# One set of score matmuls per group in layer 1 of a two-layer graph attention kernel, with k held twice

## The chip, the cores and the metric

The kernel runs on one core of a Trainium2 chip. The metric is the device time of the whole program in microseconds. The program is one launch that computes both layers. Five engines run their own instruction streams and meet at semaphores: TensorE (PE, with its weight loads shown apart as PEld), VectorE (DVE), ScalarE (ACT), GpSimd (POOL), and SyncE (SP), whose queue issues all DMAs here.

## What is computed

The input `x` has 128 graphs of 64 nodes with 768 features, `adj` a boolean 64x64 matrix per graph. Everything is fp32.

```python
# layer 0: 12 heads of 64, additive attention, gate, layer norm
h    = einsum('bnd,ade->bane', x, W);  th = tanh(h)
attn = leaky(th @ w_src + (th @ w_dst).T);  attn = where(adj, attn, -999)
feat = elu(softmax(attn) @ h + b)
gate = sigmoid(x @ H_w.T + H_b)
x    = layernorm(x + gate * feat + (1 - gate) * x)
# layer 1: 6 heads of 128, dot-product attention, layer norm
q, k, v = heads(x @ Wq + bq), heads(x @ Wk + bk), heads(x @ Wv + bv)
scores  = einsum('bhqd,bhkd->bhqk', q, k) / sqrt(128)
probs   = softmax(scores + where(adj, 0, -9e15))
x       = layernorm(x + (probs @ v merged over heads) @ Wf + bf)
```

The change concerns the scores of layer 1 and three buffers around them.

## The kernel before

Two graphs of 64 nodes fill the 128 partitions, so the input is 64 tiles of 128 tokens. `phase_a` computes layer 0 for 32 pairs of tiles, and with the product `Wv` also v of layer 1; it leaves the layer norm's rows, their transposes and v in DRAM. `phase_b` computes layer 1 for 16 groups of four tiles, two pairs `q` of two tiles `i` each. The weights of both phases use the same three SBUF tiles `w0`, `w1`, `w2`, of 7 x 3 x 384 = 8064 fp32 per partition. In `phase_b` they hold Wq, Wk and Wf, each as 15 blocks of 2 x 256 (`weight15`), 7680 of the 8064.

The products with Wq, Wk and Wf are written with 15 block products in place of 18 (`STEPS`): each step multiplies one combination of input blocks with one combination of weight blocks into one of four PSUM accumulators, and then adds the accumulator to, or subtracts it from, one or more output blocks. The combinations of the input are made by POOL: `sum_of_group` for the group's transposed input `T4` (tiles S0 to S10), `pair_sum` for the transposed contexts (tiles Sc0 to Sc10). `Stream.step` issues a step: two matmuls of 256 columns (L896), then the reads of PSUM. For q and k (`start_qk`) the first read of an output block is an ACT instruction (L917) and the further ones are DVE additions (L922). For the last product (`start_f`) all are DVE additions to the residual rows `xs` (L939). Pools rotate their buffers: a tile that is allocated again waits for the last reader of the buffer it gets.

A group takes six streams of 15 steps. Steps 0 to 59 of a group are q of the even heads (half j = 0), k of j = 0, q of j = 1, k of j = 1. In steps 60 to 89 the same positions hold the last product of the group before, first for its pair q = 0 and then for q = 1; so the streams of consecutive groups follow each other without a gap on PE. The other work is hung on step numbers by `at(step, f)`: `run` goes through the steps and calls first the dense step of that number and then the functions at it. This order is that of every engine's queue, because the whole is scheduled by hand.

For a group beginning at step o, the parts that the change touches or passes are these:

- `scores(d, 0)` at o + 32 and `scores(d, 1)` at o + 62, each two steps after the last step of that half's k. For each of three pairs of heads `nb` it allocates a PSUM tile `pb` and issues 8 matmuls (L961), one for each pair of tiles, tile and graph. Each multiplies the 128 features of 64 queries with 64 keys, and goes to the upper or lower 64 partitions.
- `scores_read` (L969) at o + 33, 35, 37 and o + 63, 65, 67 (o + 63, 64, 65 for the second half of the last group). Two DVE instructions per `nb` scale the scores, add the mask term `fill`, and write them to the softmax tiles `s0`, `s1`.
- `fill` at o + 26 makes the mask term from `adj`.
- The softmax from o + 95 (o + 66 in the last group); `probs` transposes the probabilities on PE (L1016) and ACT copies them to `pt` (L1022); `contexts` multiplies them with v (L1040) and DVE reads the result to `cT` (L1054).
- `pair_sum` (L878) for q = 0 from o + 113 and for q = 1 from o + 151, that is in steps 23 to 43 and from step 61 of the next group's numbering; `load_x` and `add_bf` (L863) bring in the residual rows; `load_T4` at step 61 and `sum_of_group` (L285) from step 66 prepare the next group.

The parts that set the order for the scores are these lines:

```python
b0 = o + (2 * j + 2) * R + 2
at(b0, lambda d=d, j=j: scores(d, j))
for nb in range(3):
    at(b0 + 1 + (1 if last and j else 2) * nb, lambda d=d, j=j, nb=nb: scores_read(d, j, nb))
```

q is allocated with two buffers and k with one, so k of the second half overwrites k of the first.

Of the kernel before, what the change touches and what calls it, by code (L numbers as in the profile page):

```python
# [9 lines left out]
F32 = mybir.dt.float32  # L10
U8 = mybir.dt.uint8
AF = mybir.ActivationFunctionType
ALU = mybir.AluOpType
AX = mybir.AxisListType

P = 128
# [45 lines left out]
def kernel(  # L62
# [31 lines left out]
    nc = tc.nc  # L94
    NB, S, D = x.shape
    A, _, E = W.shape
    HEADS = 6
    DH = D // HEADS
    NC = D // P
    HALF = D // 2  # L100
    CH = NC // 2
# [9 lines left out]
    wts = ctx.enter_context(tc.tile_pool(name="wts", bufs=1))  # L111
# [32 lines left out]
    def weight_tile(tag):  # L144
        return wts.tile([P, 7, CH, HALF], F32, name=f"w{tag}", tag=f"w{tag}")

    def weight15(i):
        return wts.tile([P, 7, CH, HALF], F32, name=f"w{i}", tag=f"w{i}").rearrange(
            "p s c o -> p (s c o)"
        )[:, : 15 * 2 * 256].rearrange("p (s c o) -> p s c o", s=15, c=2)  # L150

    def load15(wb, src, k):

# [123 lines left out]
    def group_part(d, r):  # L277

        if r < 6:
            return T4[:, :, r // 3, 2 * (r % 3) : 2 * (r % 3) + 2, :]  # L280
        return d["S"][r - 6]
# [42 lines left out]
    def phase_a(ctx):  # L324
# [470 lines left out]
        def load_early(i, src, k):  # L795
            if len(early) == i:
                early.append(weight15(i))
            load15(early[i], src, k)
# [16 lines left out]
    def phase_b(ctx, wq, wk, early_sums):  # L815
        NG = NP // 2
        k1 = ctx.enter_context(tc.tile_pool(name="l1", bufs=1))
        k3 = ctx.enter_context(tc.tile_pool(name="l3", bufs=1))
        small = ctx.enter_context(tc.tile_pool(name="lsmall", bufs=2))
        psb = ctx.enter_context(tc.tile_pool(name="psb", bufs=4, space=bass.MemoryType.PSUM))  # L820
# [15 lines left out]
            d["adj"] = a  # L836

        def fill(d):
            d["fill"] = small.tile([P, 2, 2, S], F32, name="fill1")
            nc.vector.tensor_scalar(  # L840
                d["fill"], d["adj"], 1.0, -L1_NEG, op0=ALU.subtract, op1=ALU.mult
            )
# [26 lines left out]
        def pair_part(d, q, r):  # L869

            if r < 6:
                return d["c", q, r // 3][:, 2 * (r % 3) : 2 * (r % 3) + 2, :]
            return d["Sc", q, r - 6]

        def pair_sum(d, q, k):
            r0, r1, op = SUMS[k]
            t = k1.tile([P, 2, P], F32, name=f"Sc{k}")
            nc.gpsimd.tensor_tensor(t, pair_part(d, q, r0), pair_part(d, q, r1), op)  # L878
            d["Sc", q, k] = t

# [29 lines left out]

        def start_qk(d, name, w, bias, j):

            o = k1.tile([P, 6, 2, P], F32, name=name, bufs=2 if name == "q" else 1)

            def first(b, positive, ps):
                hd = 2 * (b % 3) + j
                nc.scalar.activation(  # L917
                    o[:, b], ps, AF.Identity, bias=bias[:, hd : hd + 1], scale=1.0 if positive else -1.0
                )

            def add(b, positive, ps):
                nc.vector.tensor_tensor(o[:, b], o[:, b], ps, ALU.add if positive else ALU.subtract)  # L922

            d[name] = Stream(
                lambda r, slot, c: w[:, slot, c, j * P : (j + 1) * P],
                lambda r, slot, c: (
                    dup[:, DUP[r]] if d is st[0] and r in DUP else group_part(d, r)
                )[:, :, c, :],
                [P, 2, P],
                first,  # L930
                add,
            )
            d[name + "T", j] = o
# [13 lines left out]
            )  # L947


        def scores(d, j):  # L950
            if j == 0:
                d["s"] = [k3.tile([P, 2, HEADS, S], F32, name=f"s{q}") for q in range(2)]
            qT, kT = d["qT", j], d["kT", j]
            for nb in range(3):
                pc = psb.tile([P, 2, 2, S], F32, name="pb")
                for q in range(2):
                    for i in range(2):
                        for gr in range(2):
                            own = slice(gr * S, (gr + 1) * S)
                            b = 3 * i + nb  # L960
                            nc.tensor.matmul(  # L961
                                pc[own, q, i, :], qT[:, b, q, own], kT[:, b, q, own],
                                start=True, stop=True,
                            )
                d["pc", nb] = pc

        def scores_read(d, j, nb):
            for q in range(2):
                nc.vector.scalar_tensor_tensor(  # L969
                    d["s"][q][:, :, 2 * nb + j, :], d["pc", nb][:, q], 1.0 / math.sqrt(DH),  # L970
                    d["fill"][:, q], op0=ALU.mult, op1=ALU.add,
                )

        def sm_part(d, q, i):
            return d["s"][q][:, i]
# [36 lines left out]
        def probs(d, q, i):  # L1012

            ps = psb.tile([P, CH, P], F32, name="pb")
            for j in range(CH):
                nc.tensor.transpose(  # L1016
                    ps[:, j, :],
                    d["s"][q][:, i, 2 * j : 2 * j + 2, :].rearrange("p h m -> p (h m)"),
                    ident,
                )  # L1020
            d["pt", i] = k3.tile([P, CH, P], F32, name="pt", bufs=2)
            nc.scalar.copy(d["pt", i], ps)  # L1022

        def contexts(d, q):
# [71 lines left out]
        def at(step, *fs):  # L1096
            events.setdefault(max(step, 0), []).extend(fs)

        def at_first(step, f):

            dense.setdefault(step, []).append(f)

        R = len(STEPS)
# [21 lines left out]
        for g in range(NG):  # L1125
            d, o = st[g], N * g
            d["S"] = {} if g else early_sums
            last = g == NG - 1
            if g:
                at(o - 29 if g > 1 else 14, lambda g=g: load_T4(g))  # L1130
                at(o - 35, lambda g=g: load_adj(g))
            at(o + 26, lambda d=d: fill(d))
            ready = {}
            for k in sorted(range(len(SUMS)), key=need) if g == 0 else range(len(SUMS)):
# [6 lines left out]
                if g == 1:  # L1141

                    t = max([R * 3 + SUM_STEPS[k] + 2] + [ready[r] for r in SUMS[k][:2] if r in ready])
                    ready[6 + k] = t
                else:
                    t = o - 24 + 2 * k
# [4 lines left out]
            for j in range(2):  # L1151
                for n, (name, w, bias) in enumerate((("q", wq, bq_c), ("k", wk, bk_c))):
                    b0 = o + (2 * j + n) * R
                    at_first(b0, lambda d=d, a=(name, w, bias, j): start_qk(d, *a))
                    for i in range(R):
                        at_first(b0 + i, lambda d=d, name=name, i=i: d[name].step(i))
                b0 = o + (2 * j + 2) * R + 2
                at(b0, lambda d=d, j=j: scores(d, j))
                for nb in range(3):
                    at(b0 + 1 + (1 if last and j else 2) * nb, lambda d=d, j=j, nb=nb: scores_read(d, j, nb))  # L1160

            sm = o + 4 * R + 6 if last else o + N + 5
            for q in range(2):
                f = o + ((6 if last else 10) + q) * R
                for i in range(2):

                    t = sm + 4 * i + 13 * q if last else sm + 3 * i + 8 * q
                    at(t + (2 if last else 4), lambda g=g, q=q, i=i: load_v(g, q, i))
                    if last:
                        at(t, lambda d=d, q=q, i=i: sm_top(d, q, i, True))  # L1170
                        at(t + 2, lambda d=d, q=q, i=i: sm_top_exp(d, q, i))
                        at(t + 5, lambda d=d, q=q, i=i: sm_scale_act(d, q, i))
                        at(t + 8, lambda d=d, q=q, i=i: probs(d, q, i))
                        if i:
                            at(t + 11, lambda d=d, q=q: contexts(d, q))
                        continue
                    at(t, lambda d=d, q=q, i=i: sm_top(d, q, i))
                    at(t + 1, lambda d=d, q=q, i=i: sm_sub(d, q, i))
                    at(t + 3, lambda d=d, q=q, i=i: sm_exp(d, q, i))
                    at(t + 6, lambda d=d, q=q, i=i: sm_total(d, q, i))  # L1180
                    at(t + 7, lambda d=d, q=q, i=i: sm_scale(d, q, i))
                    at(t + 10, lambda d=d, q=q, i=i: probs(d, q, i))
                    if i:
                        at(t + 12, lambda d=d, q=q: contexts(d, q))
# [3 lines left out]
                for k in range(len(SUMS)):  # L1188
                    if q == 0:
                        t = pr + 10 + (k if last else 2 * k)  # L1190
                    else:

                        t = max(
                            [f - R + SUM_STEPS[k] + 1, pr + 10]
                            + [ready[r] for r in SUMS[k][:2] if r in ready]
                        )
# [7 lines left out]
                if last and q:  # L1204
                    for b in range(6):
                        t = f + max(i for i in range(R) if STEPS[i][5][b])
# [7 lines left out]
                for i in range(2):  # L1214
                    t = f + R + 1 + 2 * i
# [48 lines left out]
```

## Time and profile before

| | us |
|---|---|
| median of 3 runs | 2852.86 |
| lowest, highest | 2852.34, 2855.02 |
| the profiled execution | 2855.12 |
| its span from first to last instruction | 2853.3 |
| PE busy in the span | 2812.0 (99%) |
| DVE, POOL, ACT busy | 1856.9, 1543.3, 1198.7 |
| mean granted TensorE clock | 0.998 |
| one score matmul record (L961), median | 0.222 |
| one read of scores (L969), median | 0.282 |
| one addition to xs or k (L939, L922), mean | 0.42 |
| one Sc sum on POOL (L878), mean | 0.731 |

The page's times are those of one profiled execution. Its span begins and ends with an instruction, and the execution's own time is 1.8 us longer. Layer 0 takes about the first half of the span and layer 1 the rest, from about 1470 us on. A line such as `L961` is a line of the kernel. An fp32 matmul stands in the trace as two records, so the 24 matmuls of one set of scores are 48 records. Records overlap: the time a matmul adds to the stream is the distance between starts and not its own length.

### The profile page before, as it was taken

To read this page: it belongs to the slowest core of one execution; us is meant where nothing else is said; L and a number is where in the kernel's file an instruction comes from. 1 tells how busy PE (TensorE), PEld (TensorE's weight loads), DVE (VectorE), ACT (ScalarE), POOL (GpSimd) and SP (SyncE) were. 2 spreads that over 40 slices of the span, in tenths; PEclk is the share of its full clock that TensorE was granted. 3 is DMA by queue.
4 is the path that set the end of the run, shared out by engine and by line. 5 is a ranking of instruction groups with operands and counts; after the bars stand their busy time and mean duration, and the time that the engine had idled before them with its cause. 6 is when DMAs were issued, how large, how long until landed. Compare 5 with 4: busy or idle time off the path is not lost.

```text
span 2853.3 us, 50782 instructions
## 1 busy us (share of the span) xinstructions
PE 2812.0 (99%) x18108; PEld 2062.5 (72%) x18108; DVE 1856.9 (65%) x3724; ACT 1198.7 (42%) x3737; POOL 1543.3 (54%) x1653
## 2 busy tenths in 40 slices
PE   8899999999999999999999999999999999999998
PEld 5556565655655565566568888888888888888887
DVE  4887787777777777777764555555555555555556
ACT  4666656566565665665622221222211222211223
POOL 4755555655556555565536545346554456454455
PEclk9999999999999999999999999999999999999999
DMA  5434445345454454444551221212211212212222
GB/s 168 121 113 141 142 132 145 118 133 150 123 145 126 130 149 123 143 133 137 174 179 35 90 72 62 81 57 90 90 65 59 90 57 90 88 61 64 90 84 73
DMA packets 358684, 308.40 MB, mean 108 GB/s; under 512 B 226592, under 2 KB 304160, under 8 KB 358432
## 3 DMA queue, kind: packets, MB, share of 16 engines
q1 hardware_dynamic: 358432, 305.16, 35.1%
q8 instruction: 144, 2.36, 0.3%
q14 instruction: 108, 0.88, 0.1%
HBM read 191.41 MB, written 101.06 MB: 102 GB/s over the span
## 4 chain that ended last, share of the span: by engine, by line
PE 80%; DVE 8%; POOL 4%; DMA 3%; ACT 2%; issue 2%; SPq 1%; DVEq 0%; POOLq 0%; ACTq 0%
PE X L896 43%; PE X L209 31%; PE pb L1040 2%; PE pb L961 2%; DMA s<-dst_d 2%; DVE z L645 1%; PE pa L603 1%; PE pa L585 1%; DVE z L636 1%; ACT s L564 1%; POOL th L506 1%; PE pb L1016 1%; DVE st L300 1%; ACT s L548 1%; DVE xb L646 1%
## 5 line engine op out<-in xcount | busy, mean ns | idle before, releaser
L209 PE MATMUL X<-w,S 128*128 128x384 f32 x2304 | 795.2, 490 | 9.4 <-DVE v L476 3.1
L209 PEld LDWEIGHTS X<-w,S 128*128 128x128 f32 x2304 | 429.8, 190 | 297.2 <-DVE w L173 4.8
L896 PE MATMUL X<-S,w 128*128 128x256 f32 x2752 | 636.9, 380 | 0.0
L209 PE MATMUL X<-w,T 128*128 128x384 f32 x1728 | 600.3, 490 | 9.9 <-ACT snap L434 6.7
L896 PEld LDWEIGHTS X<-S,w 128*128 128x128 f32 x2752 | 516.9, 190 | 68.2
L209 PEld LDWEIGHTS X<-w,T 128*128 128x128 f32 x1728 | 326.4, 191 | 237.7 <-ACT snap L434 17.8
L878 POOL TENSOR_TENSOR Sc<-cT 128x256 f32<-128x256 f32 x224 | 162.2, 731 | 417.1 <-PE X L896 402.7
L896 PE MATMUL X<-w,Sc 128*128 128x256 f32 x1408 | 322.1, 380 | 0.3 <-POOL Sc L878 0.2
L939 DVE TENSOR_TENSOR xs<-xs,X 128x256 f32<-128x256 f32 x512 | 210.4, 419 | 168.0 <-PE X L896 160.1
L896 PEld LDWEIGHTS X<-w,Sc 128*128 128x128 f32 x1408 | 265.7, 190 | 37.9 <-DVE xs L939 0.9
L564 ACT ACTIVATE s<-s,nmx 128x64 f32<-128x64 f32 x768 | 256.1, 335 | 76.1 <-DVE nmx L559 75.2
L922 DVE TENSOR_TENSOR k<-k,X 128x256 f32<-128x256 f32 x320 | 132.7, 418 | 232.6 <-PE X L896 160.9
L922 DVE TENSOR_TENSOR q<-q,X 128x256 f32<-128x256 f32 x320 | 133.1, 419 | 199.8 <-PE X L896 159.5
L896 PE MATMUL X<-xb,w 128*128 128x256 f32 x1024 | 258.1, 382 | 0.4 <-ACT q L917 0.4
L321 ACT ACTIVATE xs<-xs,shift,rstd 128x768 f32<-128x768 f32 x62 | 63.5, 1025 | 418.7 <-POOL shift L317 412.2
L434 ACT COPY snap<-X 128x384 f32<-128x384 f32 x288 | 135.4, 470 | 230.7 <-PE X L209 227.9
L917 ACT ACTIVATE k<-X,bk_c 128x256 f32<-128x256 f32 x192 | 91.0, 474 | 315.8 <-PE X L896 315.8
L917 ACT ACTIVATE q<-X,bq_c 128x256 f32<-128x256 f32 x192 | 91.0, 474 | 298.7 <-PE X L896 298.7
L498 POOL TENSOR_TENSOR tmp<-th,wd_bc 128x768 f32<-128x768 f32 x64 | 145.2, 2268 | 131.6 <-ACT th L494 131.6
L896 PEld LDWEIGHTS X<-xb,w 128*128 128x128 f32 x1024 | 191.9, 190 | 27.9 <-ACT q L917 0.8
L548 ACT ACTIVATE s<-s,src 128x64 f32<-128x64 f32 x768 | 193.1, 335 | 31.3 <-DMA s<-dst_d 31.3
L312 POOL TENSOR_TENSOR rstd<-rstd,neg_half 128x1 f32<-128x1 f32 x126 | 69.4, 551 | 235.4 <-DVE rstd L311 234.7
(120 smaller groups left out, 4092.0 us busy)
## 6 DMA issues: line engine op xcount, KB each, us to landing
xb<-in_x_dram SPq DMA_DIRECT2D x64, 384.0 KB
s<-dst_d SPq DMA_DIRECT2D x128, 192.0 KB
x_d<-xb SPq DMA_DIRECT2D x64, 384.0 KB
xT_d<-T SPq DMA_DIRECT2D x64, 384.0 KB
v_d<-v SPq DMA_DIRECT2D x128, 192.0 KB
xb<-xT_d SPq DMA_DIRECT2D x32, 768.0 KB
xb<-v_d SPq DMA_DIRECT2D x256, 96.0 KB
xs<-x_d SPq DMA_DIRECT2D x64, 384.0 KB
```

Of the source, the lines that this page charges most:

```text
L209: nc.tensor.matmul(o, self.lhsT(i, c), rhs, start=first and c == 0, stop=last and c == CH - 1, skip_group_check=True,)
L312: nc.gpsimd.tensor_tensor(rstd, rstd, neg_half, ALU.pow)
L321: nc.scalar.activation(r, r, AF.Identity, bias=shift, scale=rstd)
L434: nc.scalar.copy(t, ps)
L498: nc.gpsimd.tensor_tensor(self.tmp, self.th, wd_bc, ALU.mult)
L548: nc.scalar.activation(self.s[:, a], self.s[:, a], AF.Prelu, bias=self.src[:, a : a + 1], alpha=LEAKY_ALPHA,)
L564: nc.scalar.activation(self.s[:, a], self.s[:, a], AF.Exp, bias=self.nmx[:, a : a + 1], accum_out=self.sm[:, a : a + 1],)
L878: nc.gpsimd.tensor_tensor(t, pair_part(d, q, r0), pair_part(d, q, r1), op)
L896: nc.tensor.matmul(ps, self.lhsT(r, slot, c), self.rhs(r, slot, c), start=start and c == 0, stop=stop and c == 1, skip_group_check=True,)
L917: nc.scalar.activation(o[:, b], ps, AF.Identity, bias=bias[:, hd : hd + 1], scale=1.0 if positive else -1.0)
L922: nc.vector.tensor_tensor(o[:, b], o[:, b], ps, ALU.add if positive else ALU.subtract)
L939: nc.vector.tensor_tensor(o, o, ps, ALU.add if positive else ALU.subtract)
```

## The change

The scores of both halves are made at o + 62 in one call. It issues, for each of the three `nb`, 16 matmuls into one PSUM tile of [128, 2, 2, 2, 64], first the 8 of j = 0 and then the 8 of j = 1. The call at o + 32 and its three reads are gone. `scores_read` at o + 63, 65, 67 (o + 63, 64, 65 in the last group) now has four DVE instructions, one for each pair of tiles and tile, each over two neighbouring heads; the mask term is broadcast over those two. k gets a second buffer; k of the first half is now read after k of the second half has been written. In the same change `fill` goes from a pool with two buffers to one buffer, `pt` (two buffers of 384) goes to the unused 384 columns of the tiles of Wq and Wk, and `Sc0` to those of Wf. The numbers of matmuls, DVE instructions, ACT copies, POOL sums and DMAs are unchanged.

```diff
@@ -144,10 +144,15 @@
     def weight_tile(tag):
         return wts.tile([P, 7, CH, HALF], F32, name=f"w{tag}", tag=f"w{tag}")
 
+    spare = {}
+
     def weight15(i):
-        return wts.tile([P, 7, CH, HALF], F32, name=f"w{i}", tag=f"w{i}").rearrange(
+        t = wts.tile([P, 7, CH, HALF], F32, name=f"w{i}", tag=f"w{i}").rearrange(
             "p s c o -> p (s c o)"
-        )[:, : 15 * 2 * 256].rearrange("p (s c o) -> p s c o", s=15, c=2)
+        )
+
+        spare[i] = t[:, 15 * 2 * 256 :]
+        return t[:, : 15 * 2 * 256].rearrange("p (s c o) -> p s c o", s=15, c=2)
 
     def load15(wb, src, k):
 
@@ -836,7 +841,7 @@
             d["adj"] = a
 
         def fill(d):
-            d["fill"] = small.tile([P, 2, 2, S], F32, name="fill1")
+            d["fill"] = k1.tile([P, 2, 2, S], F32, name="fill1")
             nc.vector.tensor_scalar(
                 d["fill"], d["adj"], 1.0, -L1_NEG, op0=ALU.subtract, op1=ALU.mult
             )
@@ -874,7 +879,10 @@
 
         def pair_sum(d, q, k):
             r0, r1, op = SUMS[k]
-            t = k1.tile([P, 2, P], F32, name=f"Sc{k}")
+            if k:
+                t = k1.tile([P, 2, P], F32, name=f"Sc{k}")
+            else:
+                t = spare[2][:, : 2 * P].rearrange("p (c n) -> p c n", n=P)
             nc.gpsimd.tensor_tensor(t, pair_part(d, q, r0), pair_part(d, q, r1), op)
             d["Sc", q, k] = t
 
@@ -910,7 +918,7 @@
 
         def start_qk(d, name, w, bias, j):
 
-            o = k1.tile([P, 6, 2, P], F32, name=name, bufs=2 if name == "q" else 1)
+            o = k1.tile([P, 6, 2, P], F32, name=name, bufs=2)
 
             def first(b, positive, ps):
                 hd = 2 * (b % 3) + j
@@ -947,29 +955,32 @@
             )
 
 
-        def scores(d, j):
-            if j == 0:
-                d["s"] = [k3.tile([P, 2, HEADS, S], F32, name=f"s{q}") for q in range(2)]
-            qT, kT = d["qT", j], d["kT", j]
+        def scores(d):
+            d["s"] = [k3.tile([P, 2, HEADS, S], F32, name=f"s{q}") for q in range(2)]
             for nb in range(3):
-                pc = psb.tile([P, 2, 2, S], F32, name="pb")
-                for q in range(2):
-                    for i in range(2):
-                        for gr in range(2):
-                            own = slice(gr * S, (gr + 1) * S)
-                            b = 3 * i + nb
-                            nc.tensor.matmul(
-                                pc[own, q, i, :], qT[:, b, q, own], kT[:, b, q, own],
-                                start=True, stop=True,
-                            )
+                pc = psb.tile([P, 2, 2, 2, S], F32, name="pb")
+                for j in range(2):
+                    qT, kT = d["qT", j], d["kT", j]
+                    for q in range(2):
+                        for i in range(2):
+                            for gr in range(2):
+                                own = slice(gr * S, (gr + 1) * S)
+                                b = 3 * i + nb
+                                nc.tensor.matmul(
+                                    pc[own, q, i, j, :], qT[:, b, q, own], kT[:, b, q, own],
+                                    start=True, stop=True,
+                                )
                 d["pc", nb] = pc
 
-        def scores_read(d, j, nb):
+        def scores_read(d, nb):
             for q in range(2):
-                nc.vector.scalar_tensor_tensor(
-                    d["s"][q][:, :, 2 * nb + j, :], d["pc", nb][:, q], 1.0 / math.sqrt(DH),
-                    d["fill"][:, q], op0=ALU.mult, op1=ALU.add,
-                )
+                for i in range(2):
+                    nc.vector.scalar_tensor_tensor(
+                        d["s"][q][:, i, 2 * nb : 2 * nb + 2, :], d["pc", nb][:, q, i],
+                        1.0 / math.sqrt(DH),
+                        d["fill"][:, q, i, None, :].to_broadcast([P, 2, S]),
+                        op0=ALU.mult, op1=ALU.add,
+                    )
 
         def sm_part(d, q, i):
             return d["s"][q][:, i]
@@ -1018,7 +1029,7 @@
                     d["s"][q][:, i, 2 * j : 2 * j + 2, :].rearrange("p h m -> p (h m)"),
                     ident,
                 )
-            d["pt", i] = k3.tile([P, CH, P], F32, name="pt", bufs=2)
+            d["pt", i] = spare[i].rearrange("p (c n) -> p c n", n=P)
             nc.scalar.copy(d["pt", i], ps)
 
         def contexts(d, q):
@@ -1154,10 +1165,10 @@
                     at_first(b0, lambda d=d, a=(name, w, bias, j): start_qk(d, *a))
                     for i in range(R):
                         at_first(b0 + i, lambda d=d, name=name, i=i: d[name].step(i))
-                b0 = o + (2 * j + 2) * R + 2
-                at(b0, lambda d=d, j=j: scores(d, j))
-                for nb in range(3):
-                    at(b0 + 1 + (1 if last and j else 2) * nb, lambda d=d, j=j, nb=nb: scores_read(d, j, nb))
+            b0 = o + 4 * R + 2
+            at(b0, lambda d=d: scores(d))
+            for nb in range(3):
+                at(b0 + 1 + (1 if last else 2) * nb, lambda d=d, nb=nb: scores_read(d, nb))
 
             sm = o + 4 * R + 6 if last else o + N + 5
             for q in range(2):
```

## The prediction

> **What bounds the kernel now.** I read the page first: engine shares, then the chain that ended last.
>
> ```profile
> PE 2812.0 (99%) x18108; PEld 2062.5 (72%) x18108; DVE 1856.9 (65%) x3724; ACT 1198.7 (42%) x3737; POOL 1543.3 (54%) x1653
> ...
> PE 80%; DVE 8%; POOL 4%; DMA 3%; ACT 2%; issue 2%; SPq 1%; DVEq 0%; POOLq 0%; ACTq 0%
> ```
>
> PE carries the time. The other engines' 18% could all be in layer 0, so the next view is the chain in order of time, cut to one group of layer 1 (start, length, what):
>
> ```profile
> 1901.42 1.55 PE pb L961 x48
> 1902.97 26.10 PE X L896 x120
> 1929.07 1.55 PE pb L961 x48
> 1930.62 37.32 PE X L896 x172
> ...
> 1987.49 1.55 PE pb L961 x48
> ```
>
> Every piece is PE. A group repeats after 1987.49 - 1901.42 = 86.07 us and holds two sets of score matmuls (L961), one per half of the heads. The waits of PE from 1475 us to the end are one line, so layer 1 is PE's own instruction stream:
>
> ```profile
> PE X L896 <- POOL Sc L878: 0.2, 1, 0.2
> ```
>
> Hence only what shortens PE's stream counts, unless another engine becomes late. What a set costs is in PE's timeline around one (start, length, line):
>
> ```profile
> 1900.40 1.03 PE L896 MATMUL X<-xb,w 128*128 128x256 f32 x4
> 1901.35 1.62 PE L961 MATMUL pb<-k,q 128*64 128x64 f32 x48
> 1902.90 2.86 PE L896 MATMUL X<-S,w 128*128 128x256 f32 x12
> 1905.60 1.03 PE L896 MATMUL X<-xb,w 128*128 128x256 f32 x4
> 1906.46 5.34 PE L896 MATMUL X<-S,w 128*128 128x256 f32 x24
> 1911.64 1.89 PE L896 MATMUL X<-xb,w 128*128 128x256 f32 x8
> ```
>
> Undisturbed, 24 records take 1911.64 - 1906.46 = 5.18 us, 0.2158 each. The four at 1900.40 would give way at 1901.26; the set begins at 1901.35 and the stream resumes at 1902.90. The twelve after it take 2.70 instead of 2.59. So a set costs (1902.90 - 1901.26) + 0.11 = 1.75 us; from the starts of single records it is 1.745 in 31 of the 32 sets. It has 48 records (24 matmuls, each in two). After the first two, their starts in the trace come in pairs 58.3 ns apart: 24 x 0.0583 = 1.40. The remaining 0.345 us is entry and exit.
>
> **What the skill says.** The Trainium skill, "TensorEngine Tiling (Array Packing)", Tiling Modes, Key Properties: changing the tiling mode drains TensorE. The scores use 128 by 64 tiles, the products around them 128 by 128, so each set changes mode twice. The trace agrees: 0.09 late at the entry, a slower first pair, 0.1 lost on the second product afterwards; no step at the borders between the set's three PSUM tiles. "PSUM — Partial Sum Buffer", The four PSUM rules: a bank holds 512 fp32 per partition. The new tile (2x2x2x64) is exactly one; no run shows it yet. "SBUF — State Buffer", Who interferes with whom: a DVE instruction with one SBUF input does not contend with GpSimd. The score read takes PSUM and one SBUF input, and POOL's sums agree: 728 ns where DVE is idle most of the time, 730 where it is busy throughout.
>
> **The change part by part.**
>
> *Scores.* 48 matmuls per group before and after. Two sets cost 2 x 1.745 = 3.49; one costs 48 x 0.0583 + 0.345 = 3.145. Saved 0.345 per group. Bounds: charging all starts evenly, the 1.398 us from first to last over 23.5 matmuls is 59.5 ns each, leaving 0.317; if mode changes cost nothing and each PSUM tile does, 0. I take 0.345: x16 = 5.52.
>
> *First group.* Its second set cost 1.861, because its second PSUM tile waited 0.12 for the last k addition (no products stand between). Now 24 matmuls, 1.4 us, precede that need: 0.12 more.
>
> *Reads of the scores.* Twelve DVE instructions per group before, twelve after, 128 elements each: nothing in sum, but all follow the second half. DVE's timeline there now:
>
> ```profile
> 1931.79 0.42 DVE L939 TENSOR_TENSOR xs<-xs,X 128x256 f32<-128x256 f32 x1 [2.26 <-PE X L896]
> 1932.12 0.48 DVE L969 SCALAR_TENSOR_TENSOR s<-pb,fill 128x128 f32<-128x128 f32 x2
> 1932.58 0.42 DVE L939 TENSOR_TENSOR xs<-xs,X 128x256 f32<-128x256 f32 x1
> 1933.44 0.42 DVE L939 TENSOR_TENSOR xs<-xs,X 128x256 f32<-128x256 f32 x1 [0.44 <-PE X L896]
> ```
>
> Two reads of 0.28 end after 0.48, so reads start c = 0.20 apart; addition to read is 0.33, last read to addition 0.26. With four reads the next addition comes at 0.33 + 3 x 0.20 + 0.26 = 1.19 instead of 0.863, 0.33 late, and the one behind it, 0.34 later, is on time. Queued behind an addition is PE: an accumulator bank is reused three steps later. The addition ending at 1932.21 frees the bank for the step at 1933.24, a margin of 1.03. So the cost is 0, hidden by that margin. In the last group the reads stand one step apart: lateness 0.33, 0.66, 0.99, still inside it, and the first softmax maximum behind them is 1 us late. Its exponentials end at 2798.0, the reciprocal that needs them stands in DVE's queue at 2799.98: 2 us cover it. Range 0 to 1 us once. The broadcast fill operand is not in the trace: bounds c = 0.20 and 0.42 (an addition of 256 elements); I take 0.20, as the elements per instruction are the same.
>
> *k twice, fill once.* k of the first half now lives to step 62 while the second half is written from step 45: with one buffer ACT's first write would wait 17 steps. With two there is no wait. fill in one buffer is written at step 26, 49 steps after its last read. Cost 0.
>
> *pt and Sc0 in the weights' spare columns.* Same instructions in the same places on ACT, POOL and PE; in the changed program's order they carry no wait on the products that read the weights. Cost 0; were ACT's copy ordered behind the products reading the weights, it would wait out a stream of 13 us, four times a group.
>
> *DMAs.* None added or moved in SP's queue. But in group 4 POOL shows:
>
> ```profile
> 1846.12 0.73 POOL L878 TENSOR_TENSOR Sc<-cT 128x256 f32<-128x256 f32 x1 [3.61 <-PE X L896]
> 1847.68 1.27 POOL L285 TENSOR_TENSOR S<-xb 128x512 f32<-128x512 f32 x1 [0.83 <-DMA xb<-xT_d]
> 1848.91 3.58 POOL L863 TENSOR_TENSOR xs<-xs,bf_bc 128x768 f32<-128x768 f32 x2
> ```
>
> The T4 load issued at step 61 landed 0.83 late, and POOL's queue then held a pair sum back until 1857.37: PE lost 0.33 there. The merged set stands between that issue and the step 64 that POOL waits for, so the load gets 3.145 - 1.745 = 1.4 us more. That stall goes: 0.33.
>
> *The earlier place.* Without the set at step 32, steps 32 to 61 come 1.745 sooner after step 31. Due there: the pair sums for q = 0, ready 33 us early, and in group 0 the second half of the Wq sums, ended by 1490.7 where 1497.9 needs them. Both hold.
>
> *Sum.* 5.52 + 0.12 + 0.33 = 5.97; I take 5.9 for a little lost at the end. The profiled execution took 2855.12 (span 2853.3), so it would become 2849.2. The three timed runs have median 2852.86 (2852.34 to 2855.02), below the profiled one by 2.26, which is between runs. From the median: 2847.0.
>
> **Rivals.**
>
> *Slower: DVE becomes late.* If a read with the broadcast operand starts every c us, the additions of steps 63 to 68 fall behind by 12c - 2.47 at the third tile, and PE stalls by what exceeds 1.03. It decides from c = 0.32, where the stall equals 0.345. At c = 0.42 it is 1.54 per group: 15 x (1.54 - 0.345) = 18 us, 2871. For it: the operand is new. Against: equal element count, 0.20 now.
>
> *No gain: the overhead belongs to each PSUM tile, not to a set.* Then only the first group's 0.12 is won: 2852.7. Against: at the borders of tiles the starts keep 52 to 58 ns.
>
> *Given back.* The last group's late DVE delays the end by 1 us, and a T4 load is late again: 5.64 - 1 = 4.6, 2848.2. For it: between 2813 and 2835 the chain runs through POOL. Against: POOL there follows PE's own steps.
>
> *More.* In ordinary runs more T4 loads are late than one: a few tenths each, 2845.5.
>
> **How the numbers follow.** Forecast 80% (its own range 2845.4 to 2848.6, with the spread of a median of a few runs), given back 9%, no gain 5%, slower 4%, more 2%. What a measurement of this kernel tells from no change is about 0.2%, 5.7 us, just under my sum: of the forecast's 80 I count 58 beyond it and 22 within. Faster 58 + 2 = 60; same 22 + 9 + 5 = 36; slower 4. Range for 8 in 10: 2845.0 to 2850.5, which takes in the given-back case.
>
> **What would show it.** One score set per group, 96 records in some 3.0 us, and a period of 85.73 us. DVE's reads in fours 0.20 apart, the addition behind them 0.33 late. No wait of PE on DVE beyond 0.1. No stall of PE on Sc in group 4, no wait of POOL on T4. Layer 0 and its hand-over as before. Wrong, if the period stays at 86.07 (overhead per tile), if reads start 0.3 apart, or if PE waits in the last group.

## The result, and the profile after

| | before | after |
|---|---|---|
| median, us (18 runs each) | 2852.93 | 2847.22 |
| lowest to highest | 2851.71 to 2855.66 | 2844.66 to 2850.76 |
| profiled execution; its span | 2855.12; 2853.3 | 2848.75; 2847.0 |
| layer 1, from the start of its first to that of its last product on PE, in the profile | 1378.81 | 1373.01 |

The ratio is 0.9978, with a 95% interval of 0.9971 to 0.9984: faster by 0.22%, the size that was forecast (2847.0). In the changed kernel L904 is what was L896, L969 was L961, L978 was L969, L947 was L939, L886 was L878, L868 was L863, L290 was L285, L1027 was L1016. In the experiments the score matmuls can also stand as L971 or L959, and their reads as L979.

The page's shares and chain look like those of before; the difference is in the pieces. The chain in order of time, over one group (start, length, what):

```profile
1924.17 2.95 PE pb L969 x96
1927.12 37.32 PE X L904 x172
1964.43 0.33 PE pb L1027 x3
```

One piece of 96 records has taken the place of two of 48, and the piece of products that used to be cut at step 32 runs through. The groups repeat after 85.72 us, where they took 86.07. PE's timeline around the set (start, length, line):

```profile
1923.14 1.03 PE L904 MATMUL X<-w,cT 128*128 128x256 f32 x4
1924.10 3.02 PE L969 MATMUL pb<-k,q 128*64 128x64 f32 x96
1927.05 2.86 PE L904 MATMUL X<-w,Sc 128*128 128x256 f32 x12
1929.74 1.03 PE L904 MATMUL X<-w,cT 128*128 128x256 f32 x4
```

Read it as before: without the set the stream would go on at 1923.14 + 0.863 = 1924.00, it goes on at 1927.05, and the twelve records after it take 2.69 in place of 2.59. That is 3.15 us; from the starts of single records it is 3.145 or 3.146 in all sixteen sets. The forecast was 3.145.

DVE's timeline behind the set:

```profile
1928.28 0.42 DVE L947 TENSOR_TENSOR xs<-xs,X 128x256 f32<-128x256 f32 x1 [3.66 <-PE X L904]
1928.62 0.88 DVE L978 SCALAR_TENSOR_TENSOR s<-pb,fill 128x128 f32<-128x128 f32 x4
1929.41 0.94 DVE L947 TENSOR_TENSOR xs<-xs,X 128x256 f32<-128x256 f32 x2
1930.28 0.88 DVE L978 SCALAR_TENSOR_TENSOR s<-pb,fill 128x128 f32<-128x128 f32 x4
```

Four reads start 0.20 apart, with the broadcast operand too, and the addition behind them comes 1.13 after the one before it: 0.27 late. POOL's timeline in group 4, where the load of T4 had been late:

```profile
1843.35 0.73 POOL L886 TENSOR_TENSOR Sc<-cT 128x256 f32<-128x256 f32 x1 [5.01 <-PE X L904]
1844.04 1.27 POOL L290 TENSOR_TENSOR S<-xb 128x512 f32<-128x512 f32 x1
1845.27 3.58 POOL L868 TENSOR_TENSOR xs<-xs,bf_bc 128x768 f32<-128x768 f32 x2
```

POOL waits 1.4 us longer for PE's step 64 (5.01 in place of 3.61), and then not at all for T4. What is left of PE's waits from 1475 us on is one line, at the very end of the last group:

```profile
PE X L904 <- DVE xs L947: 0.3, 1, 0.3
```

It stands at 2828.67, 44 us behind the last reads of scores; behind these reads PE doesn't stop.

**Where the time went.** The span fell by 6.37 us. In layer 1, 5.80: the sets of scores cost 31 x 1.7455 + 1.861 = 55.97 before and 16 x 3.1455 = 50.33 after, which is 5.64; the stall of group 4 was worth 0.43 (its period had been 86.50); against that, the stalls at the end of the last group grew from 0.43 to 0.65. These terms make 5.85, where 5.80 was measured. Layer 0, whose program is the same, happened to be 0.90 shorter in this execution, and the stretch behind the last product 0.33 longer. The first of these is chance: in the ten profiles of this document, all with the same layer 0, layer 1 begins between 1463.7 and 1470.6 us. The second is small beside that, and its cause was not looked for.

### The profile page after: what moved, and what is told of

It reads as the page before. It is cut to its first block, busy times and chain, and to the rows that moved or that the text cites. A ratio compares the mean times of both kernels' runs of the same rounds, so it can differ in the third digit from the quotient of the medians.

```text
span 2847.0 us, 50750 instructions
## 1 busy us (share of the span) xinstructions
PE 2806.6 (99%) x18108; PEld 2062.2 (72%) x18108; DVE 1853.4 (65%) x3724; ACT 1198.5 (42%) x3737; POOL 1546.6 (54%) x1653
## 4 chain that ended last, share of the span: by engine, by line
PE 87%; DVE 5%; POOL 3%; DMA 2%; ACT 2%; issue 1%; SPq 1%; DVEq 0%; ACTq 0%; POOLq 0%
PE X L904 43%; PE X L214 37%; PE pb L1051 2%; PE pb L969 2%; PE pa L608 1%; PE pa L590 1%; DMA s<-dst_d 1%; PE pb L1027 1%; ACT s L553 1%; DVE z L650 1%; ACT s L569 1%; DVE z L641 1%; DVE s L560 0%; DVE w L178 0%; POOL w L178 0%
## 5 line engine op out<-in xcount | busy, mean ns | idle before, releaser
L904 PE MATMUL X<-S,w 128*128 128x256 f32 x2752 | 635.4, 379 | 0.0
L904 PEld LDWEIGHTS X<-S,w 128*128 128x128 f32 x2752 | 518.1, 190 | 68.0
L947 DVE TENSOR_TENSOR xs<-xs,X 128x256 f32<-128x256 f32 x512 | 210.0, 419 | 175.0 <-PE X L904 166.5
L904 PE MATMUL X<-w,Sc 128*128 128x256 f32 x1280 | 294.4, 381 | 0.3 <-DVE xs L947 0.3
L904 PEld LDWEIGHTS X<-w,Sc 128*128 128x128 f32 x1280 | 241.6, 190 | 34.3 <-DVE xs L947 1.1
L904 PE MATMUL X<-xb,w 128*128 128x256 f32 x1024 | 258.0, 382 | 0.4 <-ACT q L925 0.4
L904 PEld LDWEIGHTS X<-xb,w 128*128 128x128 f32 x1024 | 192.0, 190 | 27.9 <-ACT q L925 0.8
L886 POOL TENSOR_TENSOR w<-cT 128x256 f32<-128x256 f32 x32 | 23.3, 728 | 333.6 <-PE X L904 332.4
```

Source lines behind the costliest of these rows:

```text
L904: nc.tensor.matmul(ps, self.lhsT(r, slot, c), self.rhs(r, slot, c), start=start and c == 0, stop=stop and c == 1, skip_group_check=True,)
L947: nc.vector.tensor_tensor(o, o, ps, ALU.add if positive else ALU.subtract)
```

## The experiments

The timed runs of the unchanged kernel beside these experiments had medians of 2852.9 to 2855.5, so each time is given as a ratio to the unchanged kernel's runs beside it, and the mechanism is read in the profile: the cost of a set, and the length of layer 1 from its first to its last product, which layer 0's variation doesn't touch.

### One set cut by halves, at the new place

```diff
-            at(b0, lambda d=d: scores(d))
+            parts = [[(nb, j) for nb in range(3)] for j in range(2)]
+            for n, part in enumerate(parts):
+                at(b0 + n, lambda d=d, part=part: scores(d, part))
...
-                at(b0 + 1 + (1 if last else 2) * nb, ...scores_read(d, nb))
+                at(b0 + 2 + (1 if last else 2) * nb, ...scores_read(d, nb))
```

> The changed kernel with its one set of score matmuls cut in two: the first half of the heads at step 62, the second at step 63, one product step (0.86 us) between them; buffers and reads as changed. Theory (a set costs 0.345 us of entry and exit, whatever it holds): 16 x 0.345 = 5.5 us back, 2847.2 + 5.5 = 2852.7, each set 1.745. Rival (the gain came from taking the first half away from step 32, or from the later reads): as the changed kernel, 2847.2.

Measured: 2853.99 against 2855.51, ratio 0.9995 (0.9988 to 1.0001). The forecast gives 2852.7 / 2852.93 = 0.9999, the rival 0.998. Two sets of 48 records stand around one product step, each at 1.746. (In the first group no products stand between steps 62 and 63, and the two parts run together as one set of 96 at 3.146.) The groups repeat after 86.07 again. Layer 1 takes 1378.78, 5.77 more than in the changed kernel: 15 x 0.345 = 5.18, and about 0.67 of stalls in the last group. Some 0.35 of these stand right behind the reads, which come one step later here with the softmax maximum directly after them; the rest stands at the very end, where the kernels differ anyhow. So nearly all of the gain hangs on the one product step between the halves. That the first half was taken away from step 32 gives nothing by itself.

### Three sets, and six

```diff
-            parts = [[(nb, j) for nb in range(3)] for j in range(2)]
+            parts = [[(nb, j) for j in range(2)] for nb in range(3)]    # three
+            parts = [[(nb, j)] for nb in range(3) for j in range(2)]    # six; last group: one
```

(against the cut by halves; with six sets the reads also come one step later, at 64, 66 and 68)

> The changed kernel with the 48 score matmuls of a group in three sets of 16, one for each PSUM tile, at steps 62, 63 and 64. Theory: two more entries and exits per group, 32 x 0.345 = 11.0 us, 2858.3; each set 16 x 0.0583 + 0.345 = 1.28. Rival (the overhead belongs to each PSUM tile): nothing is added, 2847.2.

> The changed kernel with six sets of 8 matmuls (tile and half) at steps 62 to 67, except in the last group, which keeps its one set. Theory, linear in the number of sets: 15 x 5 x 0.345 = 25.9 us more, 2873.1; each set 8 x 0.0583 + 0.345 = 0.81. If the entry is hidden behind the product step before it when sets are this short, less than half of that: below 2860.

Measured: three sets 2859.57, ratio 1.0014 (1.0008 to 1.0021), forecast 2858.3 / 2852.93 = 1.0019; six sets 2873.35 (four runs), ratio 1.0063 (1.0047 to 1.008), forecast 1.0071. PE's timeline with three sets:

```profile
1928.89 1.15 PE L971 MATMUL pb<-k,q 128*64 128x64 f32 x32
1929.97 1.13 PE L904 MATMUL X<-w,Sc 128*128 128x256 f32 x4
1931.04 1.15 PE L971 MATMUL pb<-k,q 128*64 128x64 f32 x32
1932.12 1.13 PE L904 MATMUL X<-w,Sc 128*128 128x256 f32 x4
1933.18 1.15 PE L971 MATMUL pb<-k,q 128*64 128x64 f32 x32
```

Sets begin 2.145 apart: 0.863 for the step between them and 1.28 for the set, as forecast; with six sets each is 0.812, forecast 0.81. Set costs by matmuls in a set are 0.812 (8), 1.279 (16), 1.746 (24), 3.146 (48): a straight line of 0.0583 per matmul with 0.345 at zero, although a group's PSUM tiles are three of the same size in all of these kernels. That rules out the rival that each tile carries the overhead. Layer 1 is 10.65 and 23.91 longer than in the changed kernel. For three sets 15 x 2 x 0.345 = 10.35, and 0.25 of stalls at the end; the expectation had counted 16 groups, but the first group's sets run together, with no products between them. For six sets 14 x 5 x 0.345 = 24.15, less 0.21 of stalls at the end: the last group keeps one set and the first group's run together again, where the expectation had counted 15 groups.

### The buffers alone

```diff
-            o = k1.tile([P, 6, 2, P], F32, name=name, bufs=2 if name == "q" else 1)
+            o = k1.tile([P, 6, 2, P], F32, name=name, bufs=2)
...
-            d["pt", i] = k3.tile([P, CH, P], F32, name="pt", bufs=2)
+            d["pt", i] = spare[i].rearrange("p (c n) -> p c n", n=P)
```

(with `fill` in one buffer and `Sc0` in `spare[2]`, as in the change)

> The kernel before with only the buffers of the change: k twice, fill once, pt and Sc0 in the weights' unused columns; scores still in two sets at steps 32 and 62. Theory (the buffers cost and give nothing): 2852.9, two sets of 1.745 per group. Rival (buffers give part of the gain, or places among the weights cost time): off by more than 1 us from 2852.9.

Measured: 2854.57 against 2855.51, ratio on record 1.0002 (0.9993 to 1.001; the quotient of the two medians is 0.9997). Of the 32 sets of 48, 31 cost 1.746, the first group's second one 1.862. In the total, the buffers neither give nor cost anything that can be measured. This kernel has the sets where the kernel before had them, and POOL again waits for T4 in three groups. The waits of POOL here:

```profile
POOL S L290 <- DMA xb<-xT_d: 1.9, 3, 1.0
```

In the kernel before it was 1.2 us, also three times. With one set (3.15 us between the load's issue and step 64), with two late ones (3.49) and with three, of which two (2.56) stand before step 64, there is no such wait. With six, of which two (1.62, less than the 1.75 of before) stand before step 64, it is 0.5 us in two cases. PE lost time to it in three groups of this execution (stalls of 0.13, 0.09 and 0.57), in one group before, and in none of the other kernels with late sets. Layer 1 is 1.33 longer here than before, and about 1.2 of that are these stalls and those at the end. That the sets before step 64 cover the load agrees with all of these profiles. How often the cover is needed, and whether the new buffers make it needed more often, one profile of each kernel can't tell.

### The same scores in the tiling mode of the products

```diff
-                        for gr in range(2):
-                            own = slice(gr * S, (gr + 1) * S)
-                            nc.tensor.matmul(pc[own, q, i, :], qT[:, b, q, own], kT[:, b, q, own], ...)
+                        nc.tensor.matmul(pc[:, q, i, :], qT[:, b, q, :], kT[:, b, q, :], ...)
```

(against the kernel before; the PSUM tile is [P, 2, 2, P], and the reads take its columns 0 to 63, so this kernel leaves out the right scores of the second graph of each tile)

> The kernel before with 128 by 128 score matmuls: all 128 tokens of a tile against each other in one matmul in place of two of 64 by 64; the reads take columns 0 to 63 for both graphs, so the second graph of a tile is scored against the first graph's keys (that part of the computation is changed). Theory (entry and exit are the change of tiling mode): a set of 12 matmuls costs 24 records x 0.108 to 0.110 = 2.6 us and no entry or exit, the first product after it is 0.22 before the second, not 0.32; total about 2852.9 + 32 x 0.87 = 2881. Rival (entry and exit belong to any foreign set of matmuls): 2.95 us a set, 2892.

Measured: 2881.12 in a single run, forecast 2881; the unchanged kernel's median beside it was 2854.40. PE's timeline around a set:

```profile
1905.84 1.03 PE L896 MATMUL X<-xb,w 128*128 128x256 f32 x4
1906.71 2.84 PE L959 MATMUL pb<-k,q 128*128 128x128 f32 x24
1909.38 2.75 PE L896 MATMUL X<-S,w 128*128 128x256 f32 x12
1911.98 0.81 PE L896 MATMUL X<-xb,w 128*128 128x256 f32 x3
```

The set begins 0.87 after the four records before it, no later than a product would; the twelve after it take 2.60, as undisturbed ones do. A set costs 2.68, which is 24 records of 0.1117, and nothing at either end. Matmuls of q with k, at the same place, into tiles of the same pool lose their entry and exit when they keep the mode of their neighbours. So a set of other matmuls has no entry and exit as such, and the 0.345 goes with the change between 128 by 64 tiles and 128 by 128. One rival is left: this edit also makes each matmul 128 columns wide in place of 64, and ends the alternation between the upper and lower 64 partitions. The kernel before does not separate these either. Its transposes (128 by 128 tiles, 128 columns) begin 0.216 after the product before them and so have no late entry; its context sets (64 by 64 tiles, 64 columns) begin 0.309 after it, like the scores. No run has a set in the products' mode with 64 columns. It is no way to a faster kernel here, since a set costs 2.68 in place of 1.746.

### Reads in smaller pieces

```diff
-                    nc.vector.scalar_tensor_tensor(
-                        d["s"][q][:, i, 2 * nb : 2 * nb + 2, :], d["pc", nb][:, q, i], ...,
-                        d["fill"][:, q, i, None, :].to_broadcast([P, 2, S]), ...)
+                    for j in range(2):
+                        nc.vector.scalar_tensor_tensor(
+                            d["s"][q][:, i, 2 * nb + j, :], d["pc", nb][:, q, i, j], ...,
+                            d["fill"][:, q, i], ...)
```

> The changed kernel with each read of the scores cut in two, one head each (8 DVE instructions of 64 elements per PSUM tile in place of 4 of 128). Theory (the reads are free only while the addition behind them is less than 1.03 us late): with starts c apart the addition comes at 0.39 + 8c, late by 8c - 0.47, and what two additions do not make good, 8c - 1.0, adds up over three tiles; for c = 0.17 that is 1.6 late and 0.6 us of PE stall per group, 2856; for c = 0.20, 1.3 per group, 2867; PE waits on DVE xs in steps 66 to 70. Rival (DVE has slack of several us): 2847.2.

Measured: 2848.22 against 2854.40, ratio 0.9977 (0.9968 to 0.9986): no slower than the changed kernel, which is the rival's number. But this run did not reach the point in dispute: the 2856 and more that were expected rested on reads 0.17 to 0.20 apart. Reads of 64 elements start 0.131 apart, so eight take 1.05 us and the addition is 0.52 late, well inside the margin. Only in the last group, where the reads follow at every step, does PE stop behind them, by 0.47. The two kernels below put the reads of every group there.

### Reads at every step

```diff
-                at(b0 + 1 + (1 if last else 2) * nb, lambda d=d, nb=nb: scores_read(d, nb))
+                at(b0 + 1 + nb, lambda d=d, nb=nb: scores_read(d, nb))
```

> The changed kernel with the reads of the three PSUM tiles behind consecutive steps (63, 64, 65) in every group, as the last group has them. Theory (an addition may be 1.03 us late before PE waits): lateness 0.33, 0.66, 0.99, no stall, 2847.2 and a group period of 85.72. If the margin is smaller than 0.9: stalls of some tenths per group, 2850 or more.

> The same with each read cut in two, one head each, whose starts are 0.131 us apart in the kernel with reads by head. Theory: additions 0.53, 1.04 and 1.55 late, PE stalls by 0.47 per group where the bank is needed (as in the last group of the kernel with reads by head), 15 x 0.47 = 7.0 us: the whole gain is eaten, 2854 to 2855, period 86.2, PE waits on DVE xs. Rival (DVE catches up unseen): 2848.

Measured: with four reads per tile 2847.38 against 2854.02, ratio 0.9979 (0.997 to 0.9988), and no stall of PE before the end of the last group. DVE's timeline there:

```profile
1926.50 0.42 DVE L947 TENSOR_TENSOR xs<-xs,X 128x256 f32<-128x256 f32 x1 [3.66 <-PE X L904]
1926.84 0.88 DVE L978 SCALAR_TENSOR_TENSOR s<-pb,fill 128x128 f32<-128x128 f32 x4
1927.63 0.41 DVE L947 TENSOR_TENSOR xs<-xs,X 128x256 f32<-128x256 f32 x1
...
1929.88 1.29 DVE L947 TENSOR_TENSOR xs<-xs,X 128x256 f32<-128x256 f32 x3
```

The addition at 1929.88 comes 3.38 after the first where three products take 2.59, so it is 0.79 late, not the 0.99 of the forecast; the two before it are 0.27 and 0.53 late. With eight, 2857.15 against 2854.02, ratio 1.0012 (1.0005 to 1.0019): the gain is gone and more. DVE's timeline of the kernel with eight, and PE's:

```profile
1928.91 0.42 DVE L947 TENSOR_TENSOR xs<-xs,X 128x256 f32<-128x256 f32 x1 [3.66 <-PE X L904]
1929.25 1.13 DVE L979 SCALAR_TENSOR_TENSOR s<-pb,fill 128x64 f32<-128x64 f32 x8
1930.30 0.41 DVE L947 TENSOR_TENSOR xs<-xs,X 128x256 f32<-128x256 f32 x1
1930.63 1.13 DVE L979 SCALAR_TENSOR_TENSOR s<-pb,fill 128x64 f32<-128x64 f32 x8
1931.69 0.41 DVE L947 TENSOR_TENSOR xs<-xs,X 128x256 f32<-128x256 f32 x1
1932.01 1.13 DVE L979 SCALAR_TENSOR_TENSOR s<-pb,fill 128x64 f32<-128x64 f32 x8
1933.07 1.26 DVE L947 TENSOR_TENSOR xs<-xs,X 128x256 f32<-128x256 f32 x3
```

```profile
1931.23 2.04 PE L904 MATMUL X<-w,Sc 128*128 128x256 f32 x8
1933.53 3.72 PE L904 MATMUL X<-w,Sc 128*128 128x256 f32 x16 [0.25 <-DVE xs L947]
```

The additions come 1.39, 1.38 and 1.38 apart where products come every 0.863: 0.53, 1.04 and 1.56 late. The last ends at 1933.48, and the product that needs its bank starts at 1933.53. PE stops twice per group, by 0.05 and 0.41 in the starts of its records, 0.47 in all, as expected. Yet the period is 86.40, not 86.2. After each stop the second product starts 0.320 after the first in place of 0.216, so a stop costs 0.105 on top of its own length: 0.47 + 2 x 0.105 = 0.68, and 85.72 + 0.68 = 86.40.

## Why the prediction was right

- *PE's own stream bounds layer 1, and nothing else shortens it.* Right: the period fell by exactly what the sets lost, 0.35.
- *A set carries 0.345 of entry and exit whatever it holds.* Right, and the term that decided: 3.145 forecast and measured, and linear from 8 to 48 matmuls. The rival that it belongs to each PSUM tile fell with the three and six sets.
- *It is the change of tiling mode.* The Trainium skill ("TensorEngine Tiling (Array Packing)", Key Properties) says that changing the tiling mode drains TensorE. It gives no price; here it would be 0.345 us for the change there and back. The kernel before agreed, and so do the scores in 128 by 128 tiles, which have no entry and no exit. That it is the mode, and not the 64 columns that went with it, is not shown apart.
- *Reads cost nothing while the addition behind them is less than 1.03 late.* Right: lateness of up to 0.79 gave no stall, 1.04 gave a first stop of 0.05, and 1.56 brought the stops to 0.47, so the edge lies between 0.79 and 1.04, as 1.03 says. The forecast's last read to addition of 0.26 was 0.20, so behind one tile's reads the lateness is 0.27 and not 0.33. The rival on the slower side is a real mechanism, not met at c = 0.20.
- *The first group gives 0.12 more.* Right: its one set costs 3.146, like the others.
- *Buffers, spare columns, the earlier place: nothing.* Right, as far as the total tells.
- *The late T4 load is covered.* Right in kind: no wait on T4 and no stall are left in this profile. Its size, 0.33, was too small: the stop cost 0.33 and then 0.105 on the next product, 0.43. The sum would have been 6.07.
- *A little lost at the end.* 0.22 of stalls more. By the letter this meets two signs that the prediction gave against itself, a wait of PE on DVE beyond 0.1 and one in the last group: there is one of 0.3. But it does not come from late reads, which these signs were meant for; PE stops at the same place in the kernel before (0.29 lost there, 0.51 here, in the starts of its records); the part of the chain there runs through the loads of the residual rows, and whether the change has a part in it stays open, since these stalls, all at the end together, are between 0.4 and 1.0 us in the other kernels.

That 2847.0 was forecast and 2847.22 measured is in part luck. The unchanged kernel's own median moved from 2852.9 to 2855.5 between series of runs, more than the 0.2 between these two, and the T4 term was 0.1 too small while the end lost 0.2 more. The gain, 0.22%, is also just above the 0.2% that the prediction took for the least that can be told from no change. The mechanism is shown by the profiles and not by the median.

## What to carry to other kernels

On a PE-bound stream, count the sets of matmuls in another tiling mode and not only the matmuls: gathering small matmuls of one mode in one place was worth a fixed amount for every set saved, here 0.345 us, provided that buffers let the first operands live so long. Before reads are gathered behind one step, work out how late the next release of an accumulator becomes, and compare it with the distance to the product that needs that bank; here, 0.79 us of lateness was free, and PE paid from 1.04 on, at a distance of 1.03.

## What the runs showed that was not expected

A stop of PE costs more than its length. After nearly every stop on a semaphore in layer 1, even one of 0.05 us, the second record started 0.320 us after the first in place of 0.216; the same 0.105 follows a set in another mode. (It was 0.291 after one stop, and 0.216 at three places in the last group where only 0.04 to 0.07 us had been lost.) The records of the weight loads suggest why. In the undisturbed stream a load starts one record ahead of its matmul; behind the stop in group 4 of the kernel before, the load starts at 1857.426 and its matmul at 1857.428, and behind the set at 1901.35 both start at 1902.90. So one weight load is no longer hidden. No run tests this reading.

And DVE reads of 64 fp32 from PSUM start 0.131 us apart against 0.198 for 128, so that halving the instructions' size cost DVE a third more and not twice as much.
